# Graph layer on one core: eleven of 782 edge batches have their rows fetched by SyncE, one row at a time

## The chip, the cores and the metric

The kernel runs on one core of one Trainium2 chip. The metric is the device time of one execution in microseconds; the median of three runs stands for the kernel. A profile is one more execution, taken with the hardware profiler: its span is the time from the first to the last instruction. Engines are named PE (matrix unit), DVE (VectorE), ACT (ScalarE), POOL (GpSimd) and SP (SyncE). SP computes nothing here, it only issues transfers; POOL issues the gathers.

## The reference

A layer norm with ReLU over 12,500 nodes of 160 numbers, then one message-passing layer over 400,000 edges, sorted by target node:

```python
h = maximum(layernorm(x), 0)
y0 = x0 @ W_l1_0 * a;  y1 = einsum(x1, W_l1_1) * a        # node rows y, 64 + 3*32 numbers
w  = silu(edge_attr_4 ... @ fc_W1) @ fc_W2                # 192 weights per edge
ys = y[edge_src]                                          # one row of y per edge
mid = products of w, ys and the edge's four numbers e0, e1
z  = zeros.at[edge_dst].add(mid)                          # sum by target node
out = x + C_S * s(h) + C_X * (z @ W_l2) * a               # s: a second linear map of h
```

What matters for this change is `y[edge_src]`: for each of 400,000 edges, a row of 160 float32 (640 bytes) is read from a table of 12,500 rows in HBM, in an order that the data gives.

## The kernel before, in words

**First stage.** Tiles of 128 nodes are normalised and mapped; the result `y` is stored to a table `y_d` in HBM by SP (line 412). `src_sb` (line 434) holds the source node of every edge, 128 edges per column: one column is an edge tile of 128 edges. There are 3125 tiles.

**Second stage.** Four tiles make a batch, so there are 782 batches (the last has one tile). The loop over `b` (lines 683 to 716) writes out, for each engine, the order of the work; for PE, ACT and DVE that order is kept as written (line 334), while POOL and SP take theirs from the framework. In pass `b`:

- `gather(b + 4)` (lines 501 to 512): POOL issues four indirect DMAs, one for each tile. Each takes a column of 128 indices and fetches 128 rows of `y_d` into one slot of the tile `yg` (128 partitions x 4 slots x 160). Six `yg` buffers exist. The first of the four carries a wait of its own: the last matmul of `sums(b)` must be done before the gather of batch `b + 4` begins ("rows keep step with the sums", line 510).
- `weigh(b + 2)`: PE and ACT make the edges' weights `pw` for a later batch (lines 539, 459, 460). Two `pw` buffers exist, so PE's matmul waits until DVE has used batch `b`'s weights up (line 472).
- `select(b + 1)` and `products(b + 1)`: DVE builds a selection matrix (lines 555, 557) and multiplies weights and fetched rows into `pr` (lines 465 to 472). Line 465 is the first that reads `yg`.
- `sums(b)`: PE adds the products up by target node (line 575), ACT moves the sums out of PSUM (lines 581, 583). Each three batches make a group whose sums PE turns, maps and adds to the nodes' accumulators (lines 591, 600, 612), and DVE adds them to `acc` (line 623), at a place read into a register (line 618).
- `features(b + 8)` (lines 302 to 312): every eighth pass SP loads the next block of edge features `xe` with eight DMAs (line 311), two buffers; the first of the eight waits until PE has read the block before last (line 519).
- every 12th pass a load of `xs` by SP (line 633), every 24th a load of `raw` (line 319).

In the second stage SP issues little more than one DMA per pass, and each SP DMA takes one of eight completion semaphores in turn and waits until the transfer that used this semaphore before has landed: at most eight are in flight.

Of the kernel before, what the change touches and what calls it, by code (L numbers as in the profile page):

```python
# [10 lines left out]
F32 = mybir.dt.float32  # L11
I32 = mybir.dt.int32
# [6 lines left out]
P = 128  # L19
M0 = 64  # L20
M1 = 32
D = M0 + 3 * M1
# [5 lines left out]
GT = 4  # L28
# [8 lines left out]
AHEAD = 4  # L37
EARLY = 8
SB = 12
LATE = 8  # L40
LO = D - P
EPS = 1e-5
C_S = math.sin(math.pi / 8.0)
# [4 lines left out]
def kernel(  # L48
# [19 lines left out]
    nc = tc.nc  # L68
    N = x.shape[0]
# [6 lines left out]
    NB = (T + GT - 1) // GT  # L76
# [4 lines left out]
    y_d = dram.tile([N, D], F32, name="y_d")  # L81
# [23 lines left out]
    at = const.tile([P, NG], F32, name="at")  # L105
# [3 lines left out]
    NQ = (NG + EG - 1) // EG  # L109
    GE = NG - LATE  # L110
    LOW = NT - LATE
    assert GE > 0 and LOW > HN
# [13 lines left out]
    wo = const.tile([P, 3, D], F32, name="wo")  # L126

    ygp = ctx.enter_context(tc.tile_pool(name="yg", bufs=6))
    ld = ctx.enter_context(tc.tile_pool(name="ld", bufs=2))
    evp = ctx.enter_context(tc.tile_pool(name="ev", bufs=2))  # L130
    rp = ctx.enter_context(tc.tile_pool(name="rel", bufs=2))
# [99 lines left out]
    def node_weight_loads():  # L231
# [5 lines left out]
        for c in range(3):  # L237
            nc.scalar.dma_start(wyr[LO + c::3, M1 * c:M1 * (c + 1)], w_l1_1)

# [4 lines left out]
    def edge_weight_loads():  # L244
# [18 lines left out]
        for c in range(3):  # L263
            nc.sync.dma_start(wsr[LO + c::3, M1 * c:M1 * (c + 1)], w_sc1)

# [36 lines left out]
    def features(b):  # L302
        blk = b * GT // BT
        if blk not in blocks:

            xe = ld.tile([P, 512], F32, name="xe")
            v = e16[blk * P:(blk + 1) * P, :].rearrange("(s k f) (h c) -> s h f k c", s=4, k=2, h=2)
            for s in range(4):
                for h in range(2):
                    lo = 32 * s + FC_IN * h  # L310
                    nc.sync.dma_start(xe[lo:lo + FC_IN, :].rearrange("p (k c) -> p k c", k=2), v[s, h])
            blocks[blk] = xe

    def e4_load(q):

        if q < NQ and q not in ev4:
            lo, hi = q * EG * TG, min((q + 1) * EG * TG, TP)
            raw = ld.tile([P, EG * TG, 4], F32, name="raw")
            nc.sync.dma_start(raw[:, :hi - lo, :].rearrange("p t c -> p (t c)"), e4[:, lo * 4:hi * 4])
            ev = evp.tile([P, EG * TG, 5], F32, name="ev")  # L320
            ev4[q] = ev, raw, lo, hi - lo

    def e4_join(q):
        if q in ev4:
            ev, raw, lo, n = ev4[q]
            evs = ev[:, :n, :].rearrange("p (q k h) c -> p h q k c", k=2, h=2)
            es = raw[:, :n, :].rearrange("p (q h k) c -> p h q k c", k=2, h=2)
            node = drel[:, lo:lo + n].rearrange("p (q h k) -> p h q k", k=2, h=2)
            for h in range(2):
                nc.scalar.activation(evs[:, h, :, :, 0:4], es[:, h], AF.Copy)  # L330
                nc.scalar.activation(evs[:, h, :, :, 4], node[:, h], AF.Copy)
# [3 lines left out]
        engines={mybir.EngineType.PE, mybir.EngineType.Activation, mybir.EngineType.DVE}))  # L335
    with (
# [44 lines left out]
        def turn_rows(q):  # L381
            m, h = steps[q][3], hs.pop(q)
            pt = nd_pt.tile([P, 2, HN, P], F32, name="pt")
            for k in range(m):
                nc.tensor.transpose(pt[:, 0, k, :], h[:, k, 0:P], ident)
                nc.tensor.transpose(pt[:, 1, k, :], h[:, k, LO:D], ident)
            pts[q] = pt
# [86 lines left out]
    with (  # L474
# [9 lines left out]
        hids, rows, wts, sels, z_ps, z_sb, zT, o_sb, prs, sums_ps, summed = ({} for _ in range(11))  # L484
        xss, hss, sTs, sps = ({} for _ in range(4))

        def tiles_of(b):
            return list(range(b * GT, min((b + 1) * GT, T)))

        def slot(t):  # L490

            return t % GT % 2 * 2 + t % GT // 2
# [8 lines left out]
        def gather(b):  # L501

            yg = ygp.tile([P, GT, D], F32, name="yg")
            rows[b] = yg
            for k, t in enumerate(tiles_of(b)):
                fetch = nc.gpsimd.indirect_dma_start(  # L506
                    out=yg[:, slot(t), :], out_offset=None, in_=y_d,
                    in_offset=bass.IndirectOffsetOnAxis(ap=src_sb[:, t:t + 1], axis=0))
                if k == 0 and b - AHEAD in summed:
                    tc.add_manual_dep(fetch.ins, summed[b - AHEAD],  # L510
                                      mybir.DependencyInfo(mybir.DependencyClass.Sync, mybir.DependencyReason.DATA),
                                      reason="rows keep step with the sums")

        def hidden(s):

            xe = blocks[s * 2 * GT // BT]
            r = slice(32 * (s % 4), 32 * (s % 4 + 1))
            ph = p_x.tile([P, 512], F32, name="px")
            nc.tensor.matmul(ph, w1[r, :], xe[r, :], start=True, stop=True)  # L519
            return ph  # L520
# [12 lines left out]
        def weigh(b):  # L533
            hT = hids[b // 2]
            pw = p_w.tile([P, GT, 256], F32, name="pw")
            n = slots_of(b)
            for k in range((n + 1) // 2):
                m, o = min(2, n), P * (b % 2 * 2 + k)
                nc.tensor.matmul(pw[:, 2 * k:2 * k + m, 0:NW], hT[:, o:o + P], w2[:, :m, :], start=True, stop=True)  # L539
            scale(pw, e4_of(b), n)  # L540
            wts[b] = pw
# [6 lines left out]
        def select(b):  # L548

            g, k = divmod(b, TG // GT)  # L550
            if k == 0:
                sels[g] = selp.tile([P, TG, 4, WN], F32, name="sel")
            n, wt = slots_of(b), wts[b]
            sel = sels[g][:, k * GT:k * GT + n, :, :]
            nc.vector.tensor_tensor(sel[:, :, 3, :], iota[:, 0:WN].unsqueeze(1).to_broadcast([P, n, WN]),  # L555
                                    wt[:, :n, NW + 3:NW + 4].to_broadcast([P, n, WN]), ALU.is_equal)
            nc.vector.tensor_tensor(sel[:, :, 0:3, :], sel[:, :, 3:4, :].to_broadcast([P, n, 3, WN]),  # L557
                                    wt[:, :n, NW:NW + 3].unsqueeze(3).to_broadcast([P, n, 3, WN]), ALU.mult)

        def products(b):  # L560
            wt, yg = wts.pop(b), rows.pop(b)
            pr = prod.tile([P, GT, PC], F32, name="pr")
            tmp = prod.tile([P, GT, 4, M1], F32, name="tmp")
            multiply(pr, tmp, wt, yg, slots_of(b))
            prs[b] = pr
# [77 lines left out]
        def skip_turn(u):  # L643
            h, m = hss.pop(u), xss[u][2]
            pt = p_x.tile([P, 2, HN, P], F32, name="px")
            for k in range(m):
                nc.tensor.transpose(pt[:, 0, k, :], h[:, k, 0:P], ident)
                nc.tensor.transpose(pt[:, 1, k, :], h[:, k, LO:D], ident)
            hT = sp.tile([P, 2, HN, P], F32, name="sT")
# [11 lines left out]
        def skip_add(u):  # L661
            _, t, m = xss.pop(u)
            ps = sps.pop(u)
            for k in range(m):
                to = acc[:, t + k, :]
                nc.vector.scalar_tensor_tensor(to, ps[:, k, :], ra[:, t + k:t + k + 1], to, op0=ALU.mult, op1=ALU.add)

        NU = (NT + HN - 1) // HN
        skips = {0: skip_load, 6: skip_center, 7: skip_turn, 10: skip_map}

        K = TG // GT
        for b in range(min(AHEAD, NB)):
            gather(b)
# [7 lines left out]
        early = [x for x in groups if x[0] < LOW]  # L681
        assert early[-1][0] + early[-1][1] == LOW and K * GE + K + len(early) <= NB
        for b in range(NB):
            g, k = divmod(b, K)
            if b + EARLY < NB:
                features(b + EARLY)
            q, r = divmod(b, EG * K)
            if r == 0:
                e4_load(q + 1)
            if r == EG * K - 4:  # L690
                e4_join(q + 1)
            u, v = divmod(b, SB)
            if b + 2 < NB:
                weigh(b + 2)
            if g:
                (turn, linear, add)[k](g - 1)
            if v in skips and u < NU:
                skips[v](u)
            if b + 1 < NB:
                select(b + 1)  # L700
                products(b + 1)
            if g and k == K - 1:
                accumulate(g - 1)
            if v == 10 and u < NU:
                skip_add(u)
            if r == EG * K - 8 and q + 1 < NQ:
                relate(rp, q + 1)
                if q + 2 == NQ:
                    any_far(rp, p_x.tile([1, 1], F32, name="px"))
            if early and b > K * GE + K - 1:  # L710
                store(*early.pop(0), nc.sync)
            sums(b)
            if b + AHEAD < NB:
                gather(b + AHEAD)
            if b % 4 == 0 and b + 4 < NB:
                hidden_pair((b + 4) // 2)
        assert NU * SB <= NB and NQ > 1
# [9 lines left out]
    with (  # L727
# [5 lines left out]
        with tc.For_i(0, n, 1) as _:  # L733
# [8 lines left out]
            with tc.For_i(0, TP // GT, 1) as g:  # L742
# [15 lines left out]
                yg = fp.tile([P, GT, D], F32, name="f_yg")  # L758
# [106 lines left out]
```

## Time and profile before

| what | value |
|---|---|
| median of 3 runs | 4045.15 us (4044.51 to 4047.3) |
| the profiled execution's own time | 4041.87 us |
| its span, first to last instruction | 4040.1 us |
| granted TensorE clock, mean | 0.969 |
| POOL busy, share of the span | 2958.0 us, 73% |
| PE busy, share of the span | 3465.7 us, 86% |
| DVE busy, share of the span | 3012.7 us, 75% |
| ACT busy, share of the span | 2665.0 us, 66% |
| mean rate of the DMA engines | 81 GB/s |

The busy share of an engine is no measure of what bounds the kernel: PE's ends are modelled, and POOL's share leaves out what it does between two gathers. The views that answer this are the one of who waited for whom (how often, how long, and the longest single wait) and the timeline, which lists single instructions with start, duration and, in brackets, the idle time before them and what ended it. A row of one line of code gives the count, the shortest, median and longest duration in ns, and the first and last start. "SPq" and "DVEq" are instructions that a sequencer carries out by itself, such as the issue of a DMA or a register load.

### The profile page before, as it was taken

To read this page: it belongs to the slowest core of one execution; us is meant where nothing else is said; L and a number is where in the kernel's file an instruction comes from. 1 tells how busy PE (TensorE), PEld (TensorE's weight loads), DVE (VectorE), ACT (ScalarE), POOL (GpSimd) and SP (SyncE) were. 2 spreads that over 40 slices of the span, in tenths; PEclk is the share of its full clock that TensorE was granted. 3 is DMA by queue.
4 is the path that set the end of the run, shared out by engine and by line. 5 is a ranking of instruction groups with operands and counts; after the bars stand their busy time and mean duration, and the time that the engine had idled before them with its cause. 6 is when DMAs were issued, how large, how long until landed. Compare 5 with 4: busy or idle time off the path is not lost.

```text
span 4040.1 us, 58241 instructions
## 1 busy us (share of the span) xinstructions
PE 3465.7 (86%) x14747; PEld 2451.6 (61%) x14747; DVE 3012.7 (75%) x8181; ACT 2665.0 (66%) x9385; POOL 2958.0 (73%) x3141
## 2 busy tenths in 40 slices
PE   7888888888888888888888888888888888888878
PEld 6566665666666665566566666566666566565556
DVE  6677777777777777777777777777777777777776
ACT  6666666666666666666666666666666666666656
POOL 0677777777777777777777777777777777777776
PEclk9999999999999999999999999999999999999999
DMA  6333333333333333333333333333332323233224
GB/s 188 84 79 77 78 77 77 75 80 77 78 77 79 75 78 78 76 79 77 76 77 79 77 78 77 77 75 80 76 77 73 76 72 76 74 76 76 72 72 139
DMA packets 246508, 327.64 MB, mean 81 GB/s; under 512 B 66600, under 2 KB 195912, under 8 KB 245912
## 3 DMA queue, kind: packets, MB, share of 16 engines
q0 software_dynamic: 150000, 256.20, 26.2%
q1 hardware_dynamic: 95446, 67.36, 5.8%
q8 instruction: 119, 1.95, 0.2%
q14 instruction: 221, 1.81, 0.1%
q10 hardware_dynamic: 722, 0.33, 0.0%
HBM read 307.62 MB, written 16.00 MB: 80 GB/s over the span
## 4 chain that ended last, share of the span: by engine, by line
DVE 26%; issue 21%; DMA 21%; PE 19%; POOL 11%; DVEq 1%; ACT 1%; SPq 0%; POOLq 0%; ACTq 0%
DMA yg<-y_d,src_sb 20%; POOL yg L506 11%; PE pw L539 8%; PE pz L575 6%; DVE tmp L467 5%; DVE tmp L465 4%; DVE pr L470 3%; DVE pr L469 2%; DVE pr L472 2%; DVE pr L468 2%; DVE acc L623 2%; PE px L519 1%; PE px L600 1%; DVE sel L555 1%; DVE sel L557 1%
## 5 line engine op out<-in xcount | busy, mean ns | idle before, releaser
L506 POOL DMA_INDIRECT yg<-y_d,src_sb x3125 | 2955.4, 946 | 1064.6 <-issue 718.3
L459 ACT ACTIVATE pw<-pw,ev 128x96 f32<-128x96 f32 x3125 | 984.8, 315 | 1072.1 <-PE pw L539 961.4
L539 PE MATMUL pw<-w,hT 128*128 128x384 f32 x3126 | 1250.0, 524 | 508.8 <-DVE pr L472 500.7
L575 PE MATMUL pz<-pr,sel 128*128 128x256 f32 x6250 | 1514.2, 386 | 0.8 <-DVE pr L472 0.8
L575 PEld LDWEIGHTS pz<-pr,sel 128*128 128x128 f32 x6250 | 1169.6, 196 | 131.5 <-PE px L591 0.9
L539 PEld LDWEIGHTS pw<-w,hT 128*128 128x128 f32 x3126 | 560.8, 195 | 1045.7 <-DVE pr L472 717.0
L465 DVE TENSOR_TENSOR tmp<-yg,pw 128x384 f32<-128x384 f32 x782 | 432.3, 553 | 849.1 <-DMA yg<-y_d,src_sb 849.0
L583 ACT ACTIVATE zs<-pz 32x64 f32<-32x64 f32 x3126 | 667.5, 214 | 41.4
L467 DVE TENSOR_REDUCE tmp<-tmp 128x128 f32<-128x384 f32 x782 | 464.3, 594 | 27.0
L557 DVE TENSOR_TENSOR sel<-sel,pw 128x384 f32<-128x384 f32 x782 | 432.7, 553 | 27.0
L470 DVE TENSOR_TENSOR pr<-pw,yg 128x384 f32<-128x384 f32 x782 | 428.7, 548 | 0.0
L581 ACT ACTIVATE zs<-pz 32x192 f32<-32x192 f32 x1042 | 337.0, 323 | 100.5 <-PE pz L575 78.5
L469 DVE TENSOR_TENSOR pr<-pw,yg 128x256 f32<-128x256 f32 x782 | 324.1, 414 | 0.0
L468 DVE TENSOR_TENSOR pr<-pw,yg 128x256 f32<-128x256 f32 x782 | 323.9, 414 | 0.0
L519 PE MATMUL px<-xe,w 32*128 32x512 f32 x782 | 278.9, 638 | 21.7 <-PE px L519 17.7
L600 PEld LDWEIGHTS px<-wo,za 128*128 128x128 f32 x1566 | 246.1, 194 | 71.1 <-issue 3.9
L524 ACT ACTIVATE hT<-px 128x512 f32<-128x512 f32 x391 | 216.2, 595 | 83.6 <-PE px L519 79.5
L600 PE MATMUL px<-wo,za 128*128 128x160 f32 x1566 | 260.4, 303 | 0.4 <-ACT za L593 0.4
L555 DVE TENSOR_TENSOR sel<-iota,pw 128x128 f32<-128x128 f32 x782 | 218.6, 279 | 47.4 <-ACT pw L460 43.1
L472 DVE TENSOR_TENSOR pr<-pw,tmp 128x128 f32<-128x128 f32 x782 | 220.4, 282 | 0.0
L612 PEld LDWEIGHTS px<-os,place 128*128 128x128 f32 x1044 | 171.8, 192 | 70.6 <-issue 2.4
L623 DVE SCALAR_TENSOR_TENSOR acc<-px,a_sb,acc 128x160 f32 x522 | 198.5, 380 | 20.8 <-PE px L612 11.5
(102 smaller groups left out, 1873.9 us busy)
## 6 DMA issues: line engine op xcount, KB each, us to landing
yg<-y_d,src_sb POOLq DMA_INDIRECT x3125
xe<-in_e SPq DMA_DIRECT2D x784, 32.0 KB
xs<-in_x SPq DMA_DIRECT2D x48, 160.0 KB
acc<-in_x SPq DMA_DIRECT2D x11, 640.0 KB
y_d<-ys SPq DMA_DIRECT2D x11, 640.0 KB
out<-acc SPq DMA_DIRECT2D x11, 640.0 KB
raw<-in_e SPq DMA_DIRECT2D x32, 192.0 KB
dst_sb<-in_dst SPq DMA_DIRECT2D x1, 1568.0 KB
```

The lines of the kernel that those rows point to most:

```text
L459: nc.scalar.activation(pw[:, k, 0:96], pw[:, k, 0:96], AF.Copy, scale=ev[:, k, 0:1])
L465: nc.vector.tensor_tensor(tmp[:, :n, 0:3, :], y1, wt[:, :n, NW:NW + 3].unsqueeze(3).to_broadcast([P, n, 3, M1]), ALU.mult)
L467: nc.vector.tensor_reduce(tmp[:, :n, 3, :], tmp[:, :n, 0:3, :].rearrange("p t c u -> p t u c"), AX.X, ALU.add)
L468: nc.vector.tensor_mul(pr[:, :n, 192:PC], wt[:, :n, 96:160], yg[:, :n, 0:M0])
L469: nc.vector.tensor_mul(pr[:, :n, 0:M0], wt[:, :n, 0:M0], yg[:, :n, 0:M0])
L470: nc.vector.tensor_mul(pr[:, :n, 96:192].rearrange("p t (c u) -> p t c u", c=3), wt[:, :n, M0:96].unsqueeze(2).to_broadcast([P, n, 3, M1]) ...
L506: fetch = nc.gpsimd.indirect_dma_start(out=yg[:, slot(t), :], out_offset=None, in_=y_d, in_offset=bass.IndirectOffsetOnAxis(ap=src_sb[:, t ...
L539: nc.tensor.matmul(pw[:, 2 * k:2 * k + m, 0:NW], hT[:, o:o + P], w2[:, :m, :], start=True, stop=True)
L557: nc.vector.tensor_tensor(sel[:, :, 0:3, :], sel[:, :, 3:4, :].to_broadcast([P, n, 3, WN]), wt[:, :n, NW:NW + 3].unsqueeze(3).to_broadcast ...
L575: mm = nc.tensor.matmul(pz[:, 0:PC], sels[g][:, t % TG // GT * GT + slot(t), :, :], pr[:, slot(t), :], start=t % WT == 0, stop=last)
L583: nc.scalar.activation(zs[:, 192 + M0 * c:192 + M0 * (c + 1)], pz[WN * c:WN * (c + 1), 192:PC], AF.Copy)
L600: nc.tensor.matmul(po[:m, :], za[:, k, :m], wo[:, k, :], start=k == 0, stop=k == 2)
```

## The change

Batches 69, 138, ... 759 (eleven of them) are taken from POOL: `gather` isn't called for them. Their 512 rows each are fetched by SP into a tile `yr` of a new pool with two buffers. In the 69 passes before such a batch is due for its gather by number, pass `v = 0` of the window issues four small DMAs that bring the 512 source indices into one partition (`at_row`), and each of the passes 0 to 63 adds one group on SP: one register load of eight indices, then for each of the eight a register instruction with two multiplications (row number to byte offset) and one DMA of one row of `y_d`, 640 bytes, into one partition of `yr`. `products` reads `yr` as it reads `yg`. The other engines' work is the same.

```diff
+RW = 69
+RS = 8
...
+    rowp = ctx.enter_context(tc.tile_pool(name="rowp", bufs=2))
...
+        def by_rows(w):
+            b = (w + 1) * RW
+            yg = rowp.tile([P, GT, D], F32, name="yr")
+            rows[b] = yg
+            at_row = rowp.tile([1, GT, P], I32, name="at_row")
+            for k, t in enumerate(tiles_of(b)):
+                nc.sync.dma_start(at_row[0:1, k, :], src[:, t:t + 1].rearrange("p o -> o p"))
+            for t in tiles_of(b):
+                for p in range(0, P, RS):
+                    yield yg, at_row, t, p
+
+        def fetch_rows(yg, at_row, t, p):
+            _, at = nc.values_load_multi_w_load_instructions(
+                at_row[0:1, t % GT, p:p + RS], engines=[mybir.EngineType.SP], min_val=0, max_val=N - 1,
+                skip_runtime_bounds_check_because="edges name nodes of the graph")
+            for j in range(RS):
+                nc.sync.dma_start(yg[p + j:p + j + 1, slot(t), :], y_d[ds(at[j], 1), :])
...
+        by_sync = set(range(RW, NB - 1, RW))
...
-            if b + AHEAD < NB:
+            if b + AHEAD < NB and (b + AHEAD) not in by_sync:
                 gather(b + AHEAD)
+            w, v = divmod(b, RW)
+            if (w + 1) * RW in by_sync:
+                if v == 0:
+                    row_of = by_rows(w)
+                if v < RW - 4:
+                    for _ in range(-(-GT * P // RS // (RW - 4))):
+                        nxt = next(row_of, None)
+                        if nxt is not None:
+                            fetch_rows(*nxt)
```

In the built program SP carries, beyond what it had, 5632 row DMAs, 44 loads of `at_row`, 704 register loads and 5632 register instructions; POOL carries 3081 gathers in place of 3125. Each row DMA waits on one of SP's eight completion semaphores like every DMA of SP; DVE's line 465 of the eleven batches waits on all eight.

## The prediction

> **What bounds the kernel now.** I read the page first, for the shares and the costliest groups.
>
> ```profile
> span 4040.1 us, 58241 instructions
> ...
> PE 3465.7 (86%) x14747; PEld 2451.6 (61%) x14747; DVE 3012.7 (75%) x8181; ACT 2665.0 (66%) x9385; POOL 2958.0 (73%) x3141
> ...
> L506 POOL DMA_INDIRECT yg<-y_d,src_sb x3125 | 2955.4, 946 | 1064.6 <-issue 718.3
> ```
>
> By these shares PE (86%) would be the bound and POOL, at 73%, would have room. But POOL's gathers are idle-separated by "issue", time in which POOL waited for nothing. So I turned to the timeline of POOL, at its first and its last gather, and to who POOL waited for.
>
> ```profile
> 116.12 1.10 POOL L506 DMA_INDIRECT yg<-y_d,src_sb  x1 [112.91 <-DMA raw<-in_e]
> ...
> 4022.27 0.95 POOL L506 DMA_INDIRECT yg<-y_d,src_sb  x1 [0.30 <-issue]
> ```
>
> ```profile
> POOL yg L506 <- issue: 718.3, 2358, 0.3
> ...
> POOL yg L506 <- PE pz L575: 18.0, 59, 0.3
> ```
>
> 3125 gathers start between 116.12 and 4022.27: (4022.27 - 116.12) / 3124 = 1.2504 us each, 5.0015 us per batch of four. The longest single wait after the first gather is 0.3 us whatever it is put down to, PE's sums (L575) among it: that 0.3 us is part of the turn, not a wait for anybody. POOL is never held up. **It is the bound**, from 116 us to 4023 us, with a turn of 0.946 + 0.304 us. The other side of it are those who wait for its rows:
>
> ```profile
> DVE tmp L465 <- DMA yg<-y_d,src_sb: 849.0, 638, 3.7
> ...
> PE pw L539 <- DVE pr L472: 500.7, 374, 4.7
> ```
>
> DVE stands idle for rows in 638 of 782 batches, 849 us in all, and PE behind it for 500.7 us. These engines would go faster if rows came faster: by about 849 / 782 = 1.1 us per batch on DVE and 500.7 / 782 = 0.64 us on PE.
>
> **The change part by part.**
>
> *POOL: what goes.* Eleven batches of four gathers: 44 x 1.2504 = 55.0 us less of the bounding engine's work, if it goes on without a wait.
>
> *Is POOL held where it skips?* After a skip, POOL is a batch, 5.0 us, early against the sums, and the first gather of each batch waits for the sums of the batch four before. Here is one batch (its gathers 421.44 to 425.19), with the first gather of the batch four later:
>
> ```profile
> 421.44 0.95 POOL L506 DMA_INDIRECT yg<-y_d,src_sb  x1 [0.30 <-DVE acc L666]
> ...
> 425.19 0.95 POOL L506 DMA_INDIRECT yg<-y_d,src_sb  x1 [0.30 <-issue]
> ```
>
> ```profile
> 427.86 0.56 DVE L465 TENSOR_TENSOR tmp<-yg,pw 128x384 f32<-128x384 f32 x1 [0.98 <-DMA yg<-y_d,src_sb]
> ```
>
> ```profile
> 430.08 0.28 DVE L472 TENSOR_TENSOR pr<-pw,tmp 128x128 f32<-128x128 f32 x1
> ...
> 432.62 1.89 PE L575 MATMUL pz<-pr,sel 128*128 128x256 f32 x8
> ...
> 441.45 0.95 POOL L506 DMA_INDIRECT yg<-y_d,src_sb  x1 [0.30 <-DVE sel L555]
> ```
>
> The sums end at 432.62 + 1.89 = 434.5 and the gather that needs them starts at 441.45: 6.9 us of room, more than the 5.0 us that a skip takes from it. The consumers must also take in one batch more per 69: PE's 0.64 us of idle per batch gains 5.0 us in 8 batches, so the room is back long before the next skip. Where the consumers run late for reasons of their own (144 of 782 batches, 18%, found their rows waiting) the room is smaller: two of eleven skips, about 2 us each. I give back 4 us of the 55 (bounds: none, by the 6.9 us; all 55, if there were no room).
>
> *SP: what comes.* The costs of this side lie beside POOL's work as long as SP keeps pace. What SP had to do before, and its waits:
>
> ```profile
> SPq L311 <- PE px L519: 2425.2, 96, 39.4
> SPq L633 <- DVE sel L555: 664.3, 48, 23.9
> SPq L319 <- ACT ev L331: 310.8, 30, 13.9
> ```
>
> 3400 us of SP's time was waiting for buffers to come free, up to 39.4 us before one burst of xe. What one issue costs there:
>
> ```profile
> 2010.89 3.59 SPq L311 DMA_DIRECT2D xe<-in_e  x8
> 2019.13 0.38 SPq L633 DMA_DIRECT2D xs<-in_x  x1
> 2028.62 0.35 SPq L319 DMA_DIRECT2D raw<-in_e  x1
> ```
>
> ```profile
> L311 SPq DMA_DIRECT2D xe<-in_e x784: 311/422/2194, 40.6 to 3956.8; - x196
> ```
>
> ```profile
> L251 SPq DMA_DIRECT2D w<-in_fc_w x8: 575/595/600, 18.8 to 23.3; - x8
> ```
>
> ```profile
> L421 SPq DMA_DIRECT2D a_sb<-in_attr x1: 582/582/582, 1.7 to 1.7; - x1
> ```
>
> ```profile
> L618 DVEq TENSOR_LOAD <-tile_i x261: 298/304/1028, 155.1 to 4030.8; - x131
> ```
>
> ```profile
> L623 DVEq FUSED_REGOPS  x1044: 53/93/104, 155.8 to 4033.8; - x174
> ```
>
> Eight xe issues back to back take 3.59 us, 0.45 us each. A row costs one issue and one register instruction of two operations, whose nearest row is the shortest on DVE, 53 ns: 0.45 + 0.05 = **0.50 us a row**. No row of the trace shows an issue whose address comes from a register, so I bound it: 0.311 + 0.053 = 0.36 us from below (the fastest issue), 0.600 + 0.053 = 0.65 us from above (the slowest small loads, taken while big loads fill the queues). I take 0.50, because the xe burst is the nearest row: small, back to back, in the same stage.
>
> The pace that it must keep, per window of 69 batches: POOL then needs 68 x 5.0015 = 340.1 us. SP has 69 xe issues x 0.45 = 31.0, some 3 of raw x 0.35 and 6 of xs x 0.38 = 3.3, four at_row loads x 0.58 = 2.3 and once their landing (2.1, below), 64 register loads x 0.304 = 19.5: 58.2 us. That leaves 281.9 us for 512 rows: **0.550 us a row is the limit**. At 0.50 SP needs 314 us and is idle for 26 us of a window: rows arrive in time, the cost is nothing. The last group of rows stands in pass 63 and is needed in pass 68, 25 us of lead. The wait that the change adds is there: DVE's first product (L465) of the eleven batches waits for SP's eight semaphores, and behind it in DVE's order stand the other products, for which PE's sums (L575) and its weights (L539) wait. While rows are in time it holds nobody; if not, it holds all three.
>
> The Trainium skill speaks against two of these terms. Its page "DMA: Bandwidth & Descriptors", section "Latency and other measured facts", gives a register load from memory a floor of about 600 ns; by that the 64 loads would take 38.4 us and the limit would fall to 0.513 us a row, just above my 0.50. This trace has 304 ns (on DVE), and the measurement decides. The same page, section "Rules for kernel authors", wants many small transfers joined into a large one, since below 64 KB most of a transfer is overhead; these are 640 bytes. By it the overhead decides the time, which is the rival below in which SP falls behind.
>
> *Transfers in flight.* SP has eight at once. The landing time shows at the end of the first stage, where the first gather above (116.12) waits for the load issued last:
>
> ```profile
> 82.57 1.77 SPq L633 DMA_DIRECT2D xs<-in_x  x2
> 87.82 25.80 SPq L412 DMA_DIRECT2D y_d<-ys  x7
> 113.71 0.35 SPq L319 DMA_DIRECT2D raw<-in_e  x1
> ```
>
> 116.12 - (113.71 + 0.35) = 2.06 us. Eight in flight with 0.35 + 2.06 us each allow a row every 0.30 us, so this limits only if landing takes over 8 x 0.55 - 0.35 = 4.0 us.
>
> *Moved past.* In the built order the first four at_row loads stand on SP between the xs issues above and the last seven stores of y_d. SP is free from 84.34 to 87.82, 3.5 us, and they need 4 x 0.58 = 2.3: nothing. If each took the 1.8 us of the biggest loads at the start, the stage would begin 4 us later. The xe, xs and raw loads behind rows wait longer for their turn, but SP reaches them up to 39.4 us early now.
>
> *DMA engines.*
>
> ```profile
> q0 software_dynamic: 150000, 256.20, 26.2%
> q1 hardware_dynamic: 95446, 67.36, 5.8%
> ```
>
> They are a third busy. The 3.6 MB of rows were moved by q0 before. Even at 16 packets a row, 5632 x 16 = 90,000 packets of q1's kind would add 5.5%, which makes gathers land later, not start later: nothing.
>
> **The sum.** 4041.87 - 55.0 + 4 = 3990.9 us in the profiled execution's own time. That execution is 3.3 us under the median of 4045.15, so the forecast is **3994 us** (own range 3984 to 4005: below, nothing given back and twice the 3 us by which the three runs differ; above, 15 us given back).
>
> **The rivals.**
>
> 1. *SP becomes the bound (slower).* Place: SP's issue of rows; it decides above 0.550 us a row. Then every window is as long as SP needs: 11 x 512 x (c - 0.550), less the 25 us of lead once. At c = 0.58 that is 169 - 25 = +144, 4138 us; at 0.60, 4251; at the upper bound of 0.65, 4532. For it: the limit is only 10% above my estimate, and a register address, or the check of it, may cost as much again as the register instruction. Against it: the first xe issue of a burst takes 311 ns and the next 422, so a pause of 53 ns between two may cost less than it lasts.
> 2. *POOL is freed but held by the sums.* The skip costs room in front of the wait on L575, and if the consumers are later than in the batch shown, half the gain goes: 4045 - 28 = 4017 us. Against it: 6.9 us of room.
> 3. *The rows' traffic lengthens POOL's turn.* Fifteen ns more on each of 3081 turns are 46 us: 4040, no change that can be told. Against it: while SP issues eight xe loads (412 to 416 us, 2011 to 2015 us) POOL keeps its 1.25 us.
>
> That the change wouldn't do what it says is not open: POOL has 3081 gathers in the built program, and no wait is added to any.
>
> **How the numbers follow.** Forecast 0.57, rival 1 0.33, rival 2 0.06, rival 3 0.04. A difference under 0.2% (8 us) is what a measurement of this kernel can't tell from none. Faster: 0.57 + 0.06 = 0.63, less 0.01 for more given back; same: rival 3 and that 0.01; slower: 0.33. The range runs from 3984 to 4250, where a row costs 0.60 us; above it lies what rival 1 has beyond that, some 0.15, and below it 0.02. The likeliest case alone has 3984 to 4005.
>
> **What would show it.** Right: POOL's gathers at 1.25 us with no wait over 0.3 us except a few of 1 to 2 us after the skips, the last gather near 3970 us, SP still waiting for PE before xe. Wrong: DVE's line 465 waiting for the row tile once in 69 batches, for tens of us, and SP with no wait before xe: the row's price is then the distance of two row DMAs on SP. A median row issue above 0.47 us without the register instruction is the point at which I am wrong.

## The result, and the profile after

The changed kernel takes 3996.68 us, median of four runs (3994.49 to 3998.79); the kernel before, run beside it, takes 4045.29 us (4044.51 to 4047.3). The ratio is 0.9879, 95% interval 0.9862 to 0.9896: 1.2% faster, 48.6 us. The forecast was 3994 us.

The profiled execution took 3994.49 us with a span of 3992.7 us, 47.4 us less than the span before. Its page opens like this (line numbers have moved: the gather is now L509, DVE's first product L468, PE's sums L597, the xe loads L314, the rows L534):

```profile
span 3992.7 us, 75854 instructions
...
PE 3457.6 (87%) x14747; PEld 2446.5 (61%) x14747; DVE 3011.2 (75%) x8181; ACT 2668.5 (67%) x9385; POOL 2919.8 (73%) x3097
...
L509 POOL DMA_INDIRECT yg<-y_d,src_sb x3081 | 2917.1, 947 | 1050.4 <-issue 696.7
```

Nothing in the shares has changed by more than a point. What changed is the count, 3081 in place of 3125, at the same duration and with the same kind of idle time. POOL's first and last gathers in the timeline:

```profile
114.52 1.10 POOL L509 DMA_INDIRECT yg<-y_d,src_sb  x1 [111.31 <-DMA yr<-y_d]
...
3969.82 0.95 POOL L509 DMA_INDIRECT yg<-y_d,src_sb  x1 [0.30 <-PE pw L561]
```

(3969.82 - 114.52) / 3080 = 1.2517 us a turn (a turn is the time from the start of one gather to the start of the next); before it was 1.2504. The view of who waited for whom (us in total, times, the longest us) says whether POOL was held anywhere, and who still waits for rows:

```profile
DVE tmp L468 <- DMA yg<-y_d,src_sb: 773.9, 590, 3.4
POOL yg L509 <- issue: 696.7, 2285, 0.3
...
PE pw L561 <- DVE pr L475: 462.3, 355, 4.2
...
POOL yg L509 <- PE pz L597: 24.5, 80, 0.4
```

After the first gather the longest wait of a gather for anything is 0.4 us, where the turn's own gap is 0.3. POOL is the bound from end to end, as before. DVE waits for rows in 590 batches in place of 638. The same view for SP's queue shows where its waiting time went:

```profile
SPq L314 <- PE px L541: 313.8, 25, 35.3
...
SPq L655 <- DVE sel L577: 30.0, 7, 27.3
```

Before, SP waited 2425.2 us ahead of xe and 664.3 us ahead of xs, besides 310.8 us ahead of raw. Now 313.8 + 30.0 us are left: SP has taken on some 3000 us of issuing. It is nearly full, but not over its limit. What the issuing consists of stands in the rows of the lines it comes from (count, then shortest/median/longest ns):

```profile
L530 SPq TENSOR_LOAD <-at_row x704: 683/782/1124, 112.2 to 3826.1; - x176
```

```profile
L534 SPq FUSED_REGOPS  x5632: 37/37/51, 113.4 to 3829.8; - x195
L534 SPq MOVE yr<-y_d x5632: 29/29/38, 113.7 to 3829.9; - x195
L534 SPq DMA_DIRECT2D yr<-y_d x5632: 224/227/323, 113.8 to 3830.0; - x195
```

And in SP's timeline between two passes with xe loads:

```profile
696.40 32.58 SPq L534 DMA_DIRECT2D yr<-y_d  x64
```

The stretch begins with the first row's issue, so it holds 64 rows and seven of their eight register loads. With the eighth, 0.78 us, it is 33.36 us, **0.521 us a row with its share of the loads**. Counted in the same way the limit is higher than the 0.550 us of the prediction, since that left the loads out: 340.1 us of a window less 38.7 us (58.2 less the loads' 19.5) are 301.4 us for 512 rows, **0.589 us a row**. SP's pace is 12% under it.

One line of the end has changed. POOL's last instruction of length is a DRAIN, here after and before:

```profile
L893 POOLq DRAIN  x3: 45/103/9293, 3982.6 to 3992.4; - x3
```

```profile
L861 POOLq DRAIN  x3: 45/103/4230, 4035.0 to 4039.8; - x3
```

It begins some 12.8 us after the last gather starts, as before, and takes 9.293 us in place of 4.230. Nothing else is behind it but the kernel's end.

With this the 47.4 us are accounted for but for 0.1 of rounding: 44 gathers at 1.2504 us, -55.0; 3080 turns at 1.35 ns more, +4.2; a first gather 1.6 us earlier, -1.6; the DRAIN, +5.1.

### The profile page after: what moved, and what is told of

Same layout as the page of the kernel before. It is cut to its first block, busy times and chain, and to the rows that moved or that the text cites. A ratio compares the mean times of both kernels' runs of the same rounds, so it can differ in the third digit from the quotient of the medians.

```text
span 3992.7 us, 75854 instructions
## 1 busy us (share of the span) xinstructions
PE 3457.6 (87%) x14747; PEld 2446.5 (61%) x14747; DVE 3011.2 (75%) x8181; ACT 2668.5 (67%) x9385; POOL 2919.8 (73%) x3097
## 4 chain that ended last, share of the span: by engine, by line
DVE 25%; PE 25%; issue 19%; DMA 18%; POOL 9%; DVEq 1%; ACT 1%; SPq 0%; POOLq 0%; ACTq 0%
DMA yg<-y_d,src_sb 18%; PE pw L561 10%; POOL yg L509 9%; PE pz L597 9%; DVE tmp L470 5%; DVE tmp L468 4%; DVE pr L473 3%; PE px L541 2%; DVE pr L472 2%; DVE pr L475 2%; DVE pr L471 2%; PE px L622 2%; DVE acc L645 2%; DVE sel L577 1%; PE px L613 1%
## 5 line engine op out<-in xcount | busy, mean ns | idle before, releaser
L509 POOL DMA_INDIRECT yg<-y_d,src_sb x3081 | 2917.1, 947 | 1050.4 <-issue 696.7
L597 PE MATMUL pz<-pr,sel 128*128 128x256 f32 x6250 | 1513.5, 386 | 0.7 <-DVE pr L475 0.7
L597 PEld LDWEIGHTS pz<-pr,sel 128*128 128x128 f32 x6250 | 1168.0, 195 | 132.4 <-PE px L613 0.9
L468 DVE TENSOR_TENSOR tmp<-yg,pw 128x384 f32<-128x384 f32 x771 | 425.9, 552 | 777.4 <-DMA yg<-y_d,src_sb 773.9
L471 DVE TENSOR_TENSOR pr<-pw,yg 128x256 f32<-128x256 f32 x771 | 319.2, 414 | 0.0
L472 DVE TENSOR_TENSOR pr<-pw,yg 128x256 f32<-128x256 f32 x771 | 318.7, 413 | 0.0
```

Of the source, the lines that this page charges most:

```text
L468: nc.vector.tensor_tensor(tmp[:, :n, 0:3, :], y1, wt[:, :n, NW:NW + 3].unsqueeze(3).to_broadcast([P, n, 3, M1]), ALU.mult)
L471: nc.vector.tensor_mul(pr[:, :n, 192:PC], wt[:, :n, 96:160], yg[:, :n, 0:M0])
L472: nc.vector.tensor_mul(pr[:, :n, 0:M0], wt[:, :n, 0:M0], yg[:, :n, 0:M0])
L509: fetch = nc.gpsimd.indirect_dma_start(out=yg[:, slot(t), :], out_offset=None, in_=y_d, in_offset=bass.IndirectOffsetOnAxis(ap=src_sb[:, t ...
L597: mm = nc.tensor.matmul(pz[:, 0:PC], sels[g][:, t % TG // GT * GT + slot(t), :, :], pr[:, slot(t), :], start=t % WT == 0, stop=last)
```

## The experiments

The theory to test: POOL's gathers set the time, each batch taken from POOL is worth four turns, and SP's rows cost nothing as long as SP's pace stays under its limit. The rivals: the rows cost something that the gain hides (their traffic, or DVE's wait); POOL is held by the sums and would gain more if it weren't; SP is the bound already.

**e1_one_load.** The eleven batches get one plain load each in place of 512 rows. It brings the rows of nodes 0 to 511 and leaves out those that the edges name.

```diff
-            at_row = rowp.tile([1, GT, P], I32, name="at_row")
...
-                    yield yg, at_row, t, p
+            nc.sync.dma_start(yg, by_tile(y_d[0:GT * P, :]))
+            return iter(())
```

> Leaves out: the rows of the eleven batches are nodes 0 to 511, brought by one plain load per batch, instead of the rows that the edges name. POOL skips the same 44 gathers, SP issues 11 loads in place of 5632 rows. Theory (POOL's turn is the bound, SP's rows are hidden): the same time as the changed kernel, 3997 us, or 4 us less if the rows' traffic is what lengthened the turn from 1.2502 to 1.2516 us. Rival (SP's rows cost the kernel something): clearly under 3990 us.

Measured: 3993.24 us (3991.87 to 3994.24), ratio 0.9878 (0.9862 to 0.9895), span 3990.1. That is the changed kernel's ratio, 0.9879, within the interval. SP waits 2341.7 us ahead of xe in this kernel, against 313.8 in the changed one, and gains nothing by it: the rows cost nothing that can be measured. The DRAIN at the end is there too:

```profile
L889 POOLq DRAIN  x3: 45/103/9293, 3980.0 to 3989.8; - x3
```

So the 9.293 us come with the smaller number of gathers and not with the rows.

**e2_rows_beside.** The reverse: SP fetches the rows as in the changed kernel, and POOL gathers all 782 batches.

```diff
-            rows[b] = yg
...
-            if b + AHEAD < NB and (b + AHEAD) not in by_sync:
+            if b + AHEAD < NB:
```

> SP fetches the same 5632 rows into a tile that nobody reads, and POOL gathers all 782 batches as before. Theory: the rows cost nothing while POOL is the bound: 4045 us, within 4 us. If the rows' traffic is what lengthens POOL's turn by 1.3 ns: 4049 us and a turn of 1.2516 us. Rival (SP's work holds other loads up): 4055 us or more, with PE waiting for xe.

Measured: 4043.93 us (4042.34 to 4044.93), ratio 1.0003 (0.9993 to 1.0013). POOL's waits and its end:

```profile
POOL yg L509 <- issue: 707.7, 2322, 0.3
...
POOL yg L509 <- PE pz L596: 25.3, 83, 0.3
```

```profile
L892 POOLq DRAIN  x3: 45/103/4230, 4036.6 to 4041.7; - x3
```

5632 row transfers beside the gathers don't lengthen POOL's turn (1.2504 us), and the DRAIN is back at 4.230 with 3125 gathers. The rival of the rows' traffic falls.

**e3_four_a_load** and **e4_sixteen_a_load.** Four and sixteen indices a register load in place of eight; the sixteen in every second pass.

```diff
-RS = 8
+RS = 4
```

```diff
-RS = 8
+RS = 16
...
-                if v < RW - 4:
+                if v < RW - 4 and v % 2 == 0:
```

> Four indices a register load instead of eight, so 1408 loads instead of 704. If a load costs 0.78 us whatever it brings, SP needs 512 x 0.41 + 128 x 0.80 + 41 = 353 us of a window of 340 us, and becomes the bound: 11 x 13 - 25 = about 120 us more than the changed kernel, 4115 us (4080 to 4150), no wait of SP before xe. If a load of four costs half as much as one of eight: 3997 us, no change.

> Sixteen indices a register load, one group of sixteen in every second pass, so 352 loads. SP needs 32 x 0.8 = 26 us less of each window if a load's price does not grow with what it brings. Theory (SP has room already): 3997 us, within 4 us, and SP's wait before xe grows by some 11 x 25 = 270 us. Rival (SP's pace still costs the changed kernel something): faster than 3990 us.

Measured: 3993.06 us (3992.94 to 3994.82), ratio 0.9878 (0.9862 to 0.9895), and 3993.87 us (3993.57 to 3994.14), ratio 0.9879 (0.9863 to 0.9896). Neither moves the time, but SP's room moves. With four a load:

```profile
L530 SPq TENSOR_LOAD <-at_row x1408: 459/554/897, 114.0 to 3855.2; - x176
```

```profile
SPq L314 <- PE px L541: 48.2, 7, 14.7
```

With sixteen:

```profile
L530 SPq TENSOR_LOAD <-at_row x352: 1132/1227/1580, 113.2 to 3809.2; - x176
```

```profile
SPq L314 <- PE px L541: 456.6, 42, 34.8
```

SP's waits ahead of xe are its room: 48.2, 313.8 and 456.6 us for four, eight and sixteen. With four a load SP has almost none left, and the time is still the same: being nearly full costs nothing, being over does. Four, eight and sixteen values take 554, 782 and 1227 ns, some 56 ns for each value more.

**e5_two_a_load** (a single execution). Two indices a load, to push SP over the limit by its pace alone.

```diff
-RS = 8
+RS = 2
```

> Two indices a register load, 2816 loads. The loads of 4, 8 and 16 took 554, 782 and 1227 ns, so 326 + 57 n, and 440 ns for two; SP's waits in those three runs put a row at 0.424 us. SP needs 512 x 0.424 + 256 x 0.485 + 41 = 382 us of a window of 340: 42 x 11 = 460 us more, less 25 to 40 us of lead once: 4425 us (4390 to 4460), and DVE waits for the row tile once in 69 batches. Rival (SP's pace is hidden whatever it is, since the transfers run on the same engines): 3993 us.

Measured: 5319.58 us, much slower than expected. SP's loads and pace:

```profile
L530 SPq TENSOR_LOAD <-at_row x2816: 633/731/1072, 112.7 to 5191.2; - x188
```

```profile
2000.53 45.60 SPq L534 DMA_DIRECT2D yr<-y_d  x56
```

A load of two takes 731 ns, more than a load of four; the expectation had 440 from the line through the others. At 45.60 / 56 = 0.814 us a row a window takes 512 x 0.814 + 38.7 = 455.5 us, eleven of them 5010; with 114 us ahead and the 22 batches behind the last window at POOL's pace (110) that is 5234 us, within 2% of the measured. So once SP is over its limit, it sets the time, as rival 1 had it. The granted clock was lower here, 0.828 against 0.969, but PE's busy time grew by only 173 us (3630.5 against 3457.6), so the clock isn't where the 1323 us come from. The wait shows in another place than the one that the prediction named first:

```profile
PE px L541 <- DMA xe<-in_e: 1365.7, 77, 22.2
POOL yg L509 <- PE pz L597: 1336.7, 169, 23.3
...
DVE tmp L468 <- DMA yr<-y_d: 166.6, 11, 30.4
```

SP hardly waited ahead of xe here, 4.6 us in all, which the prediction had named as a sign. The rows stand ahead of xe in SP's queue, so each xe block comes late, 77 times; PE waits for it, the sums are late, and POOL's gathers wait for the sums (1336.7 us). DVE's wait for the row tile, the first sign that the prediction named, is an eighth of that.

**e8_burst** (a single execution). In the loop SP gets two groups a pass in place of one, so the same 512 rows in 32 passes in place of 64.

```diff
-                    for _ in range(-(-GT * P // RS // (RW - 4))):
+                    for _ in range(2):
```

> The same rows, two groups a pass over 32 passes in place of one over 64. SP's work of a window is the same, 311 us of 340, but in 32 passes it has 32 x 9.0 = 289 us to do where they take 160. Theory (each load of xe stands behind the rows issued before it): PE waits for xe, 129 us less 25 to 65 us of lead for each of eleven windows: 4700 to 5130 us. Rival (only the sum of SP's work counts): 3995 us.

Measured: 4289.44 us.

```profile
PE px L541 <- DMA xe<-in_e: 365.0, 20, 36.5
POOL yg L509 <- PE pz L597: 320.8, 99, 32.6
```

```profile
SPq L314 <- PE px L541: 568.9, 48, 37.3
```

SP has room over a whole window (568.9 us of waiting ahead of xe), and still the kernel is 293 us slower than with even spreading, 27 us a window. The mechanism is as expected, the price less than half of the 64 to 104 us a window that was expected. One reason stands in SP's timeline. SP takes its order from the framework, and the burst that was built is shorter than the one the loop writes:

```profile
827.29 18.61 SPq L534 DMA_DIRECT2D yr<-y_d  x36
...
904.80 55.47 SPq L534 DMA_DIRECT2D yr<-y_d  x106
...
1036.32 66.20 SPq L534 DMA_DIRECT2D yr<-y_d  x128
1102.62 3.60 SPq L314 DMA_DIRECT2D xe<-in_e  x8
```

Between the xe loads of this window, eight passes apart, stand 39, 36, 34, 106, 128, 128 and 32 rows; only in the first window are there four stretches of 128. Eight passes are 40.0 us at POOL's pace, and 4.5 of them go to SP's other work by the prediction's prices, so some 68 rows fit at 0.521 us. The 158 rows above that put SP some 82 us behind. This is an estimate; as 27 us of it show, SP's lead was some 55 us, inside the 25 to 65 that the expectation took. The lost time isn't won back, since POOL's turn stays the same afterwards.

**e7_pairs.** In the manner of e1, with rows of nodes 0 to 511, two neighbouring batches are skipped, to see how much room POOL has ahead of the sums.

```diff
-            b = (w + 1) * RW
...
+            for b in ((w + 1) * RW, (w + 1) * RW + 1):
...
+                nc.sync.dma_start(yg, by_tile(y_d[0:GT * P, :]))
...
-            if b + AHEAD < NB and (b + AHEAD) not in by_sync:
+            if b + AHEAD < NB and (b + AHEAD) not in by_sync and (b + AHEAD - 1) not in by_sync:
```

> Leaves out: as in the run with one load a batch, the rows are those of nodes 0 to 511. Two batches that follow each other are taken from POOL, eleven times, 88 gathers. After a pair POOL is 10 us early against the sums and the room is 6.9 us. Theory of the room: held 3.1 us each time, 11 x 6.9 = 76 us less, a final drain of 9.3 + 44 x 0.115 = 14.4 us: 3976 us, and POOL waits for PE's sums 11 times, some 3 us. Rival (POOL is never held): 3942 us.

Measured: 3956.49 us (3952.9 to 3958.35), ratio 0.9786 (0.977 to 0.9802).

```profile
POOL yg L509 <- PE pz L593: 45.6, 87, 5.1
...
POOL yg L509 <- PE px L609: 11.1, 23, 4.4
```

Now there are waits above the turn's 0.3 us: nine, of 0.6 to 4.8 us beyond it. Of the two groups' 56.7 us, 110 turns of 0.304 us are 33.4; the rest, 23 us, is time that POOL was held. That is 2.1 us for each of eleven skips of 10.0 us, so the room is about 7.9 us on average or more, near the prediction's 6.9 us from one batch. It is uneven: seven skips are held 0.6 to 4.2 us, three for less than 0.2 or not at all, and the last 8.9 us in two waits. The time falls between the two that were expected. Of the 20 us under the 3976 us, 8.7 are the DRAIN, 5.700 us in place of the 14.4 that were expected, and 11 are holding, 23 us in place of 34. So the room is real and decides at two batches.

**e6_thirteen.** Thirteen batches, every 60th, sixteen a load, the groups spread evenly over the passes.

```diff
-RW = 69
-RS = 8
+RW = 60
+RS = 16
...
-                    for _ in range(-(-GT * P // RS // (RW - 4))):
+                    for _ in range((v + 1) * (GT * P // RS) // (RW - 4) - v * (GT * P // RS) // (RW - 4)):
```

> Thirteen batches instead of eleven (every 60th), sixteen indices a load, the groups spread evenly. SP needs 217 + 41 + 36 = 294 us of a window of 59 x 5.0 = 295 us: just in time. Theory: 8 gathers fewer than the changed kernel, 10 us less, and a drain at the end that takes 115 ns more for each gather left out, 10.2 us in place of 9.3: 3984 us. Rival (SP too slow by 5 us a window): 4040 us or more.

Measured: 4000.49 us (3998.59 to 4001.11), ratio 0.9896 (0.988 to 0.9913). POOL's last gather starts at 3959.66 us, 10 us earlier than in the changed kernel, and yet the end is later. The 13th batch is number 780, the last but one. SP's timeline there, DVE's first product of that batch, SP's one long wait and the register loads:

```profile
3944.71 1.04 SPq L294 DMA_DIRECT2D out<-acc  x2
3949.87 6.82 SPq L534 DMA_DIRECT2D yr<-y_d  x16
3956.75 0.41 SPq L294 DMA_DIRECT2D out<-acc  x1
3960.02 14.69 SPq L534 DMA_DIRECT2D yr<-y_d  x32
```

```profile
3975.87 0.55 DVE L468 TENSOR_TENSOR tmp<-yr,pw 128x384 f32<-128x384 f32 x1 [11.61 <-SPq L765]
```

```profile
SPq L294 <- DVE acc L645: 17.4, 1, 17.4
```

```profile
L530 SPq TENSOR_LOAD <-at_row x416: 1132/1227/3926, 114.2 to 3966.5; - x139
```

The stores of the result (L294) stand between the last batch's groups of rows. The first of them waits 17.4 us for accumulators that are finished late, with the rows behind it. Then each register load right behind a store is slow: of the 4.1 us between the end of the two stores at 3945.75 and the next row at 3949.87, 3.9 are one load. Seven such loads took 2.5 to 3.9 us in place of 1.23, 14 us more in all. The last 32 rows are issued up to 14 us after POOL's last gather has ended, and DVE waits 11.61 us (the view puts it down to L765, SP's next line behind the rows). By this trace the gain of two batches was lost to one queue order at the end; the run that was to test it is the next, and couldn't.

**e10_twelve, e9_every_59th, e11_again, e12_twelve_again.** To mend that: e6 without its last batch, so twelve (e10, and once more as e12); thirteen batches, every 59th, thirty-two a load, with e6's even spreading (e9); and the changed kernel beside them (e11). The first edit is made on e6, the second on the changed kernel.

```diff
-        by_sync = set(range(RW, NB - 1, RW))
+        by_sync = set(range(RW, 760, RW))
```

```diff
-RW = 69
-RS = 8
+RW = 59
+RS = 32
```

> The run with thirteen batches (every 60th) without its last one, batch 780: POOL gathers it. Theory (its loss was batch 780's rows, behind the stores at the end, and nothing in the twelve windows before): 5 us less than the changed kernel on the same chip, 15 us less than with thirteen. Rival (SP too slow in every window): no faster than the changed kernel.

> Thirteen batches, every 59th, so that the last (767) lies before the end; 32 indices a register load (estimate from the loads of 4, 8 and 16: 2.15 us), evenly spread. SP needs 217 + 16 x 2.2 + 36 = 288 us of a window of 58 x 5.0 = 290 us. Theory: 8 gathers fewer than the changed kernel and no late row: 10 us less than the changed kernel on the same chip, 0.65 us less drain. Rival (rows late at the windows' ends): not faster than the changed kernel, DVE waits for the row tile.

> The changed kernel once more, beside the two others on one chip. Expected: 0.988 of the kernel before; in the profile, POOL's turn at 1.2503 us as in the runs since and not 1.2516, a final drain of 9.3 us.

> The kernel of e10 once more, because the job in which it ran was disturbed (the kernel before took 4852 us in it): twelve batches instead of eleven have their rows fetched, one in every 60 batches, sixteen indices a load, and the last of them lies 60 batches ahead of the end, so that its rows do not stand behind the output stores as the thirteenth's did in e6. Theory (GpSimd bounds the time, each skipped batch is worth four of its turns, 5.0 us, and SyncE has room): POOL does 48 gathers fewer than the kernel before, 60.0 us, and its last gather starts near 3965 us, 5 us ahead of the changed kernel's; the time is 3985 to 3990 us by the length of the closing drain, beside 3994 to 3997 us for the changed kernel. Rival (SyncE is near its limit: 512 rows of 0.424 us and 32 loads of sixteen at 1.23 us are 256 us of a window of 60 batches, which is 300 us of POOL's pace, beside some 55 us of its other work, 311 us in all): SyncE falls 11 us a window behind, uses up its lead before xe, and PE waits for xe; then POOL's gathers wait for PE's sums in the later windows and the time is 4000 to 4090 us.

On the chip of these four runs the kernel before itself now took 4852 and 4850 us, where half an hour earlier the same chip had given 4042, so they say nothing of what twelve or thirteen batches are worth; that stays open. Measured: e10 6061.1 us, e9 6129.74, the unchanged changed kernel 5779.75 (ratio to the kernel before 1.192, 1.1886 to 1.1955), e12 6057.02. All four expectations of the time failed.

They do show the rival at work in the very kernel of the change. SP's timeline in e11, and who waited:

```profile
1035.38 57.12 SPq L534 DMA_DIRECT2D yr<-y_d  x64
```

```profile
L534 SPq DMA_DIRECT2D yr<-y_d x5632: 1/225/1403, 115.1 to 5629.9; - x195
```

```profile
POOL yg L509 <- PE pz L597: 1290.6, 178, 22.1
...
PE px L541 <- DMA xe<-in_e: 893.2, 70, 20.6
...
POOL yg L509 <- remote: 367.2, 167, 4.5
```

```profile
SPq L314 <- PE px L541: 3.7, 3, 3.0
```

The same 64 rows take 57.12 us, 0.893 us a row against the limit of 0.589. The median issue is still 225 ns, but single instructions of SP now take up to 1.4 us. At 0.893 us a window takes 512 x 0.893 + 38.7 = 495.9 us; counted as in e5 that makes 5679 us, within 2% of the span of 5774.7, and SP waits ahead of xe for 3.7 us in all. So SP, not POOL, sets the time, by the chain of e5: late xe, late sums, POOL waiting for sums. POOL's gathers themselves are unchanged (946 ns each). SP isn't the only one disturbed: waits that the view calls "remote", whose end it can put down to no instruction of this core, appear on POOL, ACT and DVE in these four runs and in none of the others. What disturbed the core, and what made the kernel before 20% slower, no run tells.

## Why the prediction was right, point by point

*The bound.* Right. POOL's turn was 1.2504 us before and between 1.2503 and 1.2517 in the changed kernel, e1, e3 and e4. e1 gets the whole gain without SP's rows, e2 none with them.

*44 gathers, -55.0 us.* Right: counted above.

*Is POOL held where it skips; 4 us given back.* The number matches the 4.2 us of the account by luck, for the mechanism wasn't at work. In the changed kernel not one gather waits over 0.4 us, so nothing is given back at the skips. The 4.2 us are a turn that was 1.35 ns longer through the whole of this execution. e1 and e3 had 1.2503 and 1.2506, so it belongs to the execution and not to the change. The mechanism itself exists: e4 has one wait of that kind.

```profile
POOL yg L509 <- PE pz L597: 24.7, 73, 2.8
```

The 2.8 us, 2.5 more than the turn's gap, come six batches after the last skip. PE had stood 5.90 us for a piece of DVE's work (L230) shortly before, so the consumers were late for a reason of their own, as the prediction had it for two of eleven skips. Without this wait e4's turn is 1.2503 us too. The room also comes back faster than by PE's 0.64 us a batch. DVE's first products around the first row batch, from DVE's timeline:

```profile
453.88 0.55 DVE L468 TENSOR_TENSOR tmp<-yg,pw 128x384 f32<-128x384 f32 x1
...
465.11 0.55 DVE L468 TENSOR_TENSOR tmp<-yr,pw 128x384 f32<-128x384 f32 x1
...
482.03 0.55 DVE L468 TENSOR_TENSOR tmp<-yg,pw 128x384 f32<-128x384 f32 x1
```

These and the five between them have no idle time in brackets, where most others wait for rows: with rows at hand the consumers take seven batches in 28.15 us, 4.02 us each, where POOL needs 5.0 for a batch. They catch up a skip in about five batches; the prediction had eight.

*The row, 0.50 us, and the load, 0.304 us.* The terms were mis-sized in opposite directions. The load takes 782 ns on SP, where I took DVE's 304. Less the loads a row takes (32.58 - 7 x 0.782) / 64 = 0.424 us, not 0.50. Of this 227 ns are the issue with an address from a register, 37 the register instruction and 29 a MOVE that I hadn't foreseen; the other 0.13 us pass between instructions and stand in no row. Together the prediction had 0.50 + 64 x 0.304 / 512 = 0.538 us a row; measured 0.521. On the load the Trainium skill was the nearer: its page "DMA: Bandwidth & Descriptors", section "Latency and other measured facts", has a floor of about 600 ns for such a load, though SP took 554 ns for four values, below it. I let a row of another engine with one value decide. Had the row really cost 0.50 and the load 0.782, SP would have been over the limit of 0.589: 0.50 + 0.098 = 0.598. The right answer was luck here: it rests on two errors that cancelled.

*The limit and rival 1.* The mechanism is right, as e5 shows, and it was nearer than the margin in the prediction said: with the load's real price all hung on the row issue. The first sign that the prediction named was the smaller one: DVE's wait for the row tile is short, PE's wait for xe long, because xe stands behind the rows in SP's queue.

*Rival 2 (held by sums)* hardly occurs with single skips (the one wait in e4) and does with double ones (e7). *Rival 3 (traffic)* falls by e2. The Trainium skill's page "DMA: Bandwidth & Descriptors", section "Rules for kernel authors", wants small transfers joined; e1 joins 512 of them into one and gains nothing that can be told (0.9878 against 0.9879), because SP's time was free. By e5 and e11 the rule holds again where it isn't.

*Transfers, landing, at_row.* Right where they could be read. SP waited 1.3 us in all for rows of its own in flight (in e9 to e12 64 to 81 us). Queue q1 rises by 17,600 packets, not the 90,000 of the upper bound:

```profile
q0 software_dynamic: 147888, 252.59, 25.6%
q1 hardware_dynamic: 113046, 71.01, 6.4%
```

The first gather starts at 114.52 us, before it was 116.12, so the at_row loads that were moved past the stores delayed nothing.

*Not foreseen.* The closing DRAIN, +5.1 us. In the forecast's own execution time, 3990.9 us against 3994.49, it is the largest term that was missing. That the sum came so near is luck too: the 4 us given back, which did not come at the skips, stood in its place.

## What to carry to other kernels

Look for the engine whose gap between two instructions is always the same (here 0.3 us) and whose longest wait is no longer: that one is the bound, at whatever busy share, and each piece of work taken from it is worth its full turn until a wait of the others exceeds their room. An idle queue can take such work, but its margin is to be counted per window, register loads included, and whatever stands behind the new work in that queue (here xe) is the first to suffer. So does the new work itself behind something that waits, as e6's rows did behind the result's stores. Spread the work evenly over the passes, and look in the trace whether the built order does so: two groups a pass in place of one cost 293 us with the same total.

## What the runs showed of the hardware

- A register load on SP took 554, 782 and 1227 ns for 4, 8 and 16 values, about 56 ns a value, and 731 ns for 2: a load of two was slower than one of four, not only in sum. Right behind a store of the result, loads of 16 took 2.5 to 3.9 us (e6).
- Issuing a 640-byte row at an address from a register took 227 ns (median of 5632), half of the 422 ns of a 32-KB xe load in the same stage. From one row to the next it is 0.42 us all the same, with the register instruction, the MOVE and the time between, against 0.45 us for xe.
- The length of POOL's closing DRAIN goes with how many gathers the kernel has issued, not with pace or time: 9.293 us after 3081 gathers, in kernels with spans from 3990.1 (e1) to 5774.7 us (e11); 8.967 after 3077 (e10, e12); 8.640 after 3073 (e6, e9); 5.700 after 3037 (e7). That is 0.082 us more for each gather. After 3125 it is 4.230, so between 3081 and 3125 it falls back; where, no run shows. Counts at which it is short are worth some microseconds.
